# Queries and keys of two batch entries in seven block products of eight, in a decoder layer written out by slots

## The chip, the cores and the metric

The kernel runs on one core of one Trainium2 chip. The core has a tensor engine (TensorE, "PE" in a profile, with its weight loads listed as "PEld"), a vector engine (VectorE, DVE), a scalar engine (ScalarE, ACT), GpSimd (POOL), and a queue that issues most DMAs (SyncE, SP). [...] The metric is device time in microseconds (us); lower is better.

## The reference

The reference is one pre-norm decoder layer on 16 batch entries of 128 tokens with 256 features, all in float32. Cut to what matters:

```
x = x + self_attention(layernorm(x))            # 16 heads of 64, biases on Q, K, V and output
x = x + cross_attention(layernorm(x), context)  # 16 heads of 16, keys masked
x = x + experts(layernorm(x))                   # 8 experts of 512, all computed, scaled by a gate

Q = einsum('btd,hkd->bthk', x, W_Q) + b_Q       # 256 features -> 16 * 64 = 1024
K = einsum('btd,hkd->bthk', x, W_K) + b_K
scores = einsum('bqhk,bshk->bhqs', Q, K) / 8
```

The change concerns Q and K of the self attention. In the kernel they are needed transposed: 1024 rows, as 8 chunks of 128, by 128 tokens of an entry. The 256 features are two blocks of 128, so a chunk of one entry is the sum of two 128x128x128 products: 16 products for the queries of an entry and 16 for its keys.

## The kernel before

**Stages.** A first part computes both attentions entry by entry; a second one computes the experts over 2048 tokens in four groups of 512. Between them lies a short tail that finishes the cross attention of the last two entries and computes some hidden values of the first expert. The expert part already forms its products in the seven-of-eight manner, with the helpers `combined` (sums of weight blocks) and `right` (differences of token blocks).

**Slots.** The first part is a pipeline of 16 slots, one per batch entry. Slot `s` does the self attention of entry `s`, most of the cross attention of entry `s - 1`, the end of that of `s - 2`, the norm for the experts of `s - 3`, and the projections (queries, keys, values) of entry `s + 1`. Slots 0 to 2 lack the parts whose entry would be negative. Slot 15 has no next entry; six steps `pre_hidden` (two matmuls of 512 columns each, hidden values of the first expert) stand in the places of the projections there.

**What sets the order.** The order on PE, DVE, ACT and POOL is written out by hand. Each step has a name with a due time in the table `DUE` (for slot 0 some have another in `FIRST_DUE`). A step of slot `s` is due at `s * SLOT + DUE[name]`. All steps are put in one heap and issued by due time; an engine then executes its instructions strictly in that order. The due times are only an order, the real times are made by the chip. SP's DMAs are not under this table's order of engines, but are issued where the steps call them.

The names that the prediction uses, with what they do:

- `S0`, `S1`: scores of the two halves of the heads (line 465). `max0`, `max1`: their maxima, on DVE (line 351). `ex0a`, `ex0b`, `ex1a`, `ex1b`: the exponentials, on ACT (line 357), four heads each. `r..`: reciprocals of the sums, on DVE (line 368). `mul..`: the products with them, on POOL (line 372).
- `T1a1` to `T1b2`: transposes of the probabilities on PE (line 387), with a copy out of PSUM, named with a final `e`. `T2..`: the same for the cross attention of entry `s - 2`.
- `SVa`, `SVb`: probabilities times values; `atT0`, `atT1`: their evictions with a bias, on DVE. `SO`: the output projection; `xsSO`: its addition to the residual `xs`, on DVE. `bn`, `root`: statistics and inverse root; `xn`, `xn3`: normalised rows for the cross attention and for the experts. `LNx`, `LN3`, `LN1`: their transposes on PE; `LNxc`, `LN3c`, `LN1c`: the copies on ACT. `xn1`: normalised rows for the next self attention. `st0` to `st11`: statistics of entries 4 to 15, taken in slot 0; `late`: their roots. `ab..`: addition of an output bias to `xs`, on POOL.
- `cvr`, `ck`, `CQ`, `CS`, `CV`, `CO`: value rows, keys, queries, scores, values and output of the cross attention; `msk0`, `msk1`: its masks, on DVE; `c` before a softmax name marks the cross attention's (`cmax0`, `cex0a`). `cvre`, `cke`, `q2T`, `at2T`, `xsCO`: their evictions. `cross`: some small set-up for it in slot 0.
- `q0`, `q1`, `k0`, `k1`: queries and keys of entry `s + 1`, chunks 0 to 3 and 4 to 7 (line 410); `q0e`, `q1e` evict the queries on DVE, `ke0`, `ke1` the keys on ACT. `v0`, `v1`: the values (line 449), `ve0`, `ve1` their copies on ACT.

**PSUM.** All results of matmuls except scores are put in tiles of one bank from the pool `ps_mm`, which has four:

```
ps_mm = both.enter_context(
    tc.tile_pool(name="ps_mm", bufs=4, space=bass.MemoryType.PSUM, side="right")
)
```

The four are handed out in turn, so a step that takes a new tile needs the tile of four allocations earlier to have been read. Scores have a pool of their own with two tiles of two banks.

**Weights.** `wq`, `wk` and `wv` lie in the buffers `k0`, `k1` and `k2` of the pool `keep`, whose fourth one, `k3`, is unused until the first `pre_hidden`. Two of four parts of the experts' first weights (`w1_0`, `w1_1`) are loaded at the start.

Of the kernel before, what the change touches and what calls it, by code (L numbers as in the profile page):

```python
# [18 lines left out]
P = 128  # L19
# [32 lines left out]
SLOT = 28.2  # L52
DUE = dict(
    S0=0.0, S1=1.0, max0=1.2, LNx=2.0, cvr=2.22, max1=2.34, LNxc=2.42, ex0a=2.72, T2b1=3.09,
    T2b2=3.53, T2b1e=3.72, q0=3.96, cvre=4.09, T2b2e=4.32, ex0b=4.44, r0a=4.92, mul0a=5.2,
    T2a1=5.7, ex1a=5.81, q0e=5.9, T2a2=6.14, r0b=6.5, k0=6.57, T2a1e=6.63, mul0b=6.78, ex1b=7.19,
    T2a2e=7.23, r1a=7.83, mul1a=8.11, CQ=8.31, ke0=8.56, r1b=8.76, mul1b=9.13, v0=9.18, q2T=9.38,
    xn1=10.44, T1a1=10.9, ab1=11.04, ve0=11.1, T1a2=11.34, T1a1e=11.54, T1b1=11.77, T1a2e=12.14,
    T1b2=12.21, LN1=12.64, T1b1e=12.74, LN1c=13.06, CS=13.08, T1b2e=13.34, msk0=14.23, SVa=14.25,
    SVb=15.15, atT0=15.42, msk1=16.02, CV=16.15, q1=17.2, atT1=17.21, at2T=17.81, cmax0=18.15,  # L60
    LN3=18.94, SO=19.16, q1e=19.29, LN3c=19.36, cex0a=19.66, cmax1=19.89, cex0b=21.03,
    cr0a=21.36, cmul0a=22.23, cex1a=22.4, cr0b=22.6, CO=22.61, xsSO=22.81, bn=23.22,
    cmul0b=23.25, v1=23.47, xsCO=23.72, cex1b=23.78, cr1a=24.06, bn3=24.19, cmul1a=24.34,
    root=24.79, k1=25.19, ve1=25.39, ke1=27.13, cr1b=27.14, ck=27.19, xn=27.27,
    cmul1b=27.42, xn3=27.77, cke=28.26, ab2=28.44, early0=6.65, early1=6.7, early=7.9,
    cross=13.9, st0=14.3, st1=14.8, st2=15.6, st3=16.2, st4=17.4, st5=17.9, st6=18.4, st7=18.9,
    st8=20.0, st9=20.5, st10=21.0, st11=21.5, late=31.7,
)

FIRST_DUE = dict(  # L70
    fk0=-11.4, fq0=-9.5, fk0e=-9.4, fq0e=-7.7, fk1=-7.2, norm1=-7.0, S0=-5.4, fk1e=-5.3, fq1=-4.4,
    max0=-4.0, ex0a=-2.7, fLN=-2.65, fq1e=-2.6, fv0=-2.3, fLNc=-1.4, r0a=-1.32, ex0b=-1.3,
    mul0a=-1.2, S1=-0.6, fv0e=0.1, r0b=0.15, mul0b=0.2, max1=0.4, fv1=0.41, ex1a=1.65, fv1e=3.0,
    r1a=3.1, mul1a=3.2, ex1b=3.6, cvre=5.0, r1b=5.1, mul1b=5.2, fab0=5.5, fab1=6.5,
)
PRE_STEPS = ("q0", "k0", "v0", "q1", "v1", "k1")
# [4 lines left out]
def decoder_layer(  # L81
# [147 lines left out]
    for i in range(2):  # L229
        load_w1(i, we1)  # L230


    bk1 = const.tile([P, C1], F32, tag="bk1", name="bk1")
    xnT = const.tile([P, KD, NT], F32, tag="xnT", name="xnT")
# [148 lines left out]
    def transposed(w, prT, n, name):  # L383

        tr = psum_mm("tr_p").rearrange("p (j t) -> p j t", j=4)
        for j in range(4):
            nc.tensor.transpose(tr[:, j, :], w["pr"][:, 4 * n + j, :], ident)  # L387
        due(name, nc.vector.tensor_copy, prT[:, 4 * n : 4 * n + 4, :], tr)
# [7 lines left out]
    def self_norm_transposed(b, name="LN1c"):  # L396
        xnT1 = ap.tile([P, KD, 1, T], F32, tag="xnT1", name="xnT1")
        transpose_tokens([entry.pop(("xn1", b))], xnT1, name)
        entry["xnT1", b] = xnT1

    def project(b, w, n, tag):

        mm = psum_mm("mm_qk").rearrange("p (c t) -> p c t", c=4)
        if n == 0:
            entry[tag, b] = ap.tile([P, C1, T], F32, tag=tag, name=tag)
        xnT1 = entry["xnT1", b]
        for i in range(4):
            c = 4 * n + i
            for k in range(KD):
# [3 lines left out]
                    xnT1[:, k, 0, :],  # L413
# [3 lines left out]
        return entry[tag, b], mm  # L417

    def queries(b, n, name="q{}e"):
# [4 lines left out]
            qT[:, 4 * n : 4 * n + 4, :],  # L424
# [33 lines left out]
    def self_scores(b, half):  # L458

        qT, kT = entry["qT", b], entry["kT", b]  # L460
        sc = psum_sc("sc1")
        for c in range(4):
            for j in range(2):
# [3 lines left out]
                    qT[r, 4 * half + c, :],  # L467
                    kT[r, 4 * half + c, :],
# [314 lines left out]
    def slot(s):  # L783
# [23 lines left out]
        if s + 2 < B:  # L807
            at("xn1", self_norm, s + 2)
            at("ab1", add_bias, s + 2, BO1)
            at("LN1", self_norm_transposed, s + 2)  # L810
        if s + 1 < B:
            for n in range(2):
                at(f"q{n}", queries, s + 1, n)
                at(f"k{n}", keys, s + 1, n)
                at(f"v{n}", values, s + 1, n)
        else:
            for n, name in enumerate(PRE_STEPS):
                copy = nc.vector.tensor_copy if name[0] == "q" else nc.scalar.copy
                out = f"q{name[1]}e" if name[0] == "q" else f"{name[0]}e{name[1]}"
                at(name, pre_hidden, n, copy, out)  # L820
        if s == 0:
            for n in range(2):
# [3 lines left out]
                at(f"fab{n}", add_bias, n, BO1)  # L826

# [5 lines left out]
            at("fLN", self_norm_transposed, 1, "fLNc")  # L833
# [447 lines left out]
```

## Time and profile before

| | us |
|---|---|
| median of 3 runs | 867.79 (867.68 to 867.98) |
| the profiled execution | 868.2 |
| its span, first to last instruction | 866.1 |
| first `S0` of slot 0, of slot 1, of slot 2 | 13.39, 42.70, 67.17 |
| `S0` of slots 14 and 15 | 403.13, 430.93 |
| end of slot 15 | 458.36 |

Times inside the span count from its start. In a group of instructions, "x16" counts instructions of the engine; a float32 product of 128x128 weights is two of them on PE, so 8 products are x16. Busy times of neighbouring instructions overlap a little: the time that one takes in a dense row is read from start to start. A line of a timeline gives the start, the duration, the engine, the line of the kernel, the operation, what it writes and reads, the shape, the count, and in brackets the idle time before it with what ended that.

### The profile page before, as it was taken

To read this page: it belongs to the slowest core of one execution; us is meant where nothing else is said; L and a number is where in the kernel's file an instruction comes from. 1 tells how busy PE (TensorE), PEld (TensorE's weight loads), DVE (VectorE), ACT (ScalarE), POOL (GpSimd) and SP (SyncE) were. 2 spreads that over 40 slices of the span, in tenths; PEclk is the share of its full clock that TensorE was granted. 3 is DMA by queue.
4 is the path that set the end of the run, shared out by engine and by line. 5 is a ranking of instruction groups with operands and counts; after the bars stand their busy time and mean duration, and the time that the engine had idled before them with its cause. 6 is when DMAs were issued, how large, how long until landed. Compare 5 with 4: busy or idle time off the path is not lost.

```text
span 866.1 us, 15987 instructions
## 1 busy us (share of the span) xinstructions
PE 856.7 (99%) x5962; PEld 718.1 (83%) x5962; DVE 627.8 (72%) x1517; ACT 429.1 (50%) x1629; POOL 166.5 (19%) x179
## 2 busy tenths in 40 slices
PE   8999999999999999999999999999999999999997
PEld 7888888888888888888875557888888888888886
DVE  4887787778878787878777587786656766576656
ACT  3365765567565755576554713343344334343342
POOL 5133423343233423343321100000000000000000
PEclk9999999999999999999999999999999999999999
DMA  8700000000000000000041100000000000000000
GB/s 228 250 2 14 2 13 2 2 13 2 13 2 2 13 2 2 14 2 2 28 173 45 48 1 1 1 13 13 0 1 1 25 1 0 1 13 13 1 0 25
DMA packets 18318, 21.29 MB, mean 25 GB/s; under 512 B 9585, under 2 KB 13697, under 8 KB 17601
## 3 DMA queue, kind: packets, MB, share of 16 engines
q1 hardware_dynamic: 17728, 19.93, 7.3%
q8 instruction: 47, 0.77, 0.4%
q0 software_dynamic: 368, 0.30, 0.2%
q14 instruction: 31, 0.25, 0.1%
q10 hardware_dynamic: 144, 0.04, 0.0%
HBM read 18.16 MB, written 2.10 MB: 23 GB/s over the span
## 4 chain that ended last, share of the span: by engine, by line
PE 90%; DVE 6%; ACT 1%; DMA 1%; issue 1%; SPq 0%; POOL 0%; DVEq 0%; POOLq 0%
PE y L1025 19%; PE mm_qk L410 12%; PE mm_o L509 6%; PE tr_p L387 6%; PE mm_v L449 6%; PE he L1025 5%; PE hf L1025 5%; PE ha L1025 5%; PE sc L465 4%; PE po L489 3%; PE mm_h L773 3%; PE hb L1025 3%; PE sc L599 2%; PE po L638 2%; PE y L915 2%; PE mm_q L577 2%
## 5 line engine op out<-in xcount | busy, mean ns | idle before, releaser
L372 POOL TENSOR_TENSOR cpr<-cpr,rinv 128x512 f32<-128x512 f32 x64 | 68.5, 1071 | 220.2 <-DVE rinv L368 219.8
L357 ACT ACTIVATE cpr<-sc,nmax 128x128 f32<-128x128 f32 x256 | 89.9, 411 | 11.6 <-DVE nmax L351 11.6
L357 ACT ACTIVATE pr<-sc,nmax 128x128 f32<-128x128 f32 x256 | 90.9, 418 | 2.6 <-DVE nmax L351 2.6
L372 POOL TENSOR_TENSOR pr<-pr,rinv 128x512 f32<-128x512 f32 x64 | 65.8, 1040 | 74.0 <-DVE rinv L368 73.2
L351 DVE TENSOR_REDUCE nmax<-sc 128x8 f32<-128x1024 f32 x64 | 76.5, 1216 | 1.0 <-PE sc L465 1.0
L1054 ACT ACTIVATE h<-u,colv 128x256 f32<-128x256 f32 x56 | 28.4, 508 | 93.6 <-DVE u L1041 91.7
L1055 DVE TENSOR_TENSOR c<-u,hf 128x256 f32<-128x256 f32 x56 | 23.5, 420 | 69.3 <-PE hf L1025 69.1
L278 ACT COPY xnT<-tr_x 128x256 f32<-128x256 f32 x43 | 16.0, 373 | 109.2 <-PE tr_x L336 109.2
L410 PEld LDWEIGHTS mm_qk<-xnT,wk 128*128 128x128 f32 x512 | 60.9, 192 | 8.4 <-issue 4.1
L1025 PE MATMUL hf<-xt,w 128*128 128x256 f32 x224 | 66.8, 380 | 0.4 <-DVE u L1040 0.4
L1025 PE MATMUL ha<-xnT,w 128*128 128x256 f32 x224 | 66.6, 379 | 0.0
L1025 PE MATMUL y<-t,w 128*128 128x256 f32 x224 | 66.6, 380 | 0.0
L357 ACT ACTIVATION_READ_ACCUMULATOR pr<-sc,nmax 128x1 f32 x256 | 65.9, 257 | 0.0
L357 ACT ACTIVATION_READ_ACCUMULATOR cpr<-sc,nmax 128x1 f32 x256 | 64.4, 252 | 0.0
L410 PE MATMUL mm_qk<-xnT,wq 128*128 128x128 f32 x512 | 64.0, 278 | 0.0
L410 PE MATMUL mm_qk<-xnT,wk 128*128 128x128 f32 x512 | 62.5, 275 | 0.9 <-ACT xnT L262 0.5
L1038 ACT COPY u<-ha 128x256 f32<-128x256 f32 x56 | 20.9, 372 | 84.9 <-PE ha L1025 84.9
L410 PEld LDWEIGHTS mm_qk<-xnT,wq 128*128 128x128 f32 x512 | 59.8, 192 | 3.1 <-issue 2.9
L449 PE MATMUL mm_v<-wv,xnT 128*128 128x512 f32 x128 | 60.3, 593 | 0.0
L509 PE MATMUL mm_o<-wo,atT 128*128 128x256 f32 x256 | 57.9, 379 | 0.0
L1025 PE MATMUL y<-h,w 128*128 128x256 f32 x224 | 57.6, 379 | 0.0
L278 DVE COPY prT<-tr_p 128x512 f32<-128x512 f32 x64 | 39.7, 682 | 19.3 <-PE tr_p L387 19.3
(174 smaller groups left out, 1879.8 us busy)
## 6 DMA issues: line engine op xcount, KB each, us to landing
w<-in_w SPq DMA_DIRECT2D x8, 1024.0 KB, 5.5
ctx<-in_ctxT SPq DMA_DIRECT2D x8, 256.0 KB, 2.7
out_x<-ot SPq DMA_DIRECT2D x8, 256.0 KB, 2.1
xs<-in_x SPq DMA_DIRECT2D x3, 512.0 KB, 5.2
wk<-in_wk SPq DMA_DIRECT2D x2, 512.0 KB, 6.9
wq<-in_wq SPq DMA_DIRECT2D x2, 512.0 KB, 7.7
wv<-in_wv SPq DMA_DIRECT2D x2, 512.0 KB, 9.7
wo<-in_wo SPq DMA_DIRECT2D x1, 1024.0 KB, 8.9
```

The costliest lines, as they stand in the source:

```text
L278: f(*a)
L351: nc.vector.tensor_reduce(w["nmax"], sc, AX.X, ALU.max, negate=True)
L357: nc.scalar.activation(w["pr"][:, i, :], sc[:, i, :], AF.Exp, bias=w["nmax"][:, i : i + 1], scale=1.0, accum_out=sums[:, j : j + 1],)
L372: nc.gpsimd.tensor_tensor(four, four, w["rinv", n].unsqueeze(2).broadcast_to([P, 4, T]), ALU.mult)
L387: nc.tensor.transpose(tr[:, j, :], w["pr"][:, 4 * n + j, :], ident)
L410: nc.tensor.matmul(mm[:, i, :], w[:, k, c * P : (c + 1) * P], xnT1[:, k, 0, :], start=(k == 0), stop=(k == KD - 1),)
L449: nc.tensor.matmul(mm, entry["xnT1", b][:, k, 0, :], wv[:, k, f], start=(k == 0), stop=(k == KD - 1),)
L465: nc.tensor.matmul(sc[:, j, c * T : (c + 1) * T], qT[r, 4 * half + c, :], kT[r, 4 * half + c, :], start=True, stop=True,)
L489: nc.tensor.matmul(po[j * DH1 : (j + 1) * DH1, c, :], v[:, h * DH1 : (h + 1) * DH1], prT[:, 4 * j + c, :], start=True, stop=True,)
L509: nc.tensor.matmul(mm[:, :D], atT[:, c, :], wo[:, c, :], start=(c == 0), stop=(c == C1 - 1))
L1025: nc.tensor.matmul(out, left[p // q][n - 1][:, p % q], rights[n - 1], **flags)
L1054: nc.scalar.activation(h[:, 1, 1], u[:, 3], AF.Gelu, bias=col(B1 + 2 * p + 1))
```

## The change

Queries and keys of entries 0 and 1 are projected as before. From entry 2 on two entries `b0` and `b0 + 1` are projected together. For the four chunks of one half, the two chunk parities and the two feature blocks form a 2x2 matrix of 128x128 weight blocks (for each of two pairs of chunks), the two feature blocks and the two entries a 2x2 matrix of token blocks. Their product, eight block products, is formed from seven, with sums of weight blocks made once in slot 0 (`weight_sums`, steps `w0` and `w1`; the sums need the weights changed in place, and the keys' scale is put into the weights) and differences of token blocks made once per pair (`pair_factors`, step `tf`).

Slot `s` does half `s % 2` of the pair that begins at `s + 2 - s % 2`: 14 products for queries and 14 for keys, in slots 0 to 13. The seven products lie in two banks: products 1 and 6 in the halves `a` and `b` of one, 7 and 5 in `f` and `e` of the other; products 2, 4 and 3 are added to `a`, `f` and `e` later. The steps on PE are `q1x`, `q1y`, `q2x`, `q2y` and the same with `k`. Their sums are formed on ACT (`qu0`, `qc00`: two pieces of 128x128 each) and DVE (`qu1`, `qu2`, `qu3`, `qc1` of 128x256, `qc0` as two of 128x128).

The norms and transposes for the next self attention are done for two entries in every second slot. The four `T1` copies move from DVE to ACT. The value projection `v1` comes before `v0`, the cross and expert steps have new places, and `SLOT` becomes 27.34 with 7.5 more for slot 0. Slot 0 does the plain queries and keys of entry 1, both weight sums and the first half of the pair (2, 3). Two of the six early hidden steps move from slot 15 to slot 14. The sums lie in the unused buffer `k3` and in the buffer of `w1_1`, whose load is therefore issued in slot 14. The pool of normalised rows has 4 buffers instead of 6. `qT` and `kT` become half tiles with three and two buffers.

```diff
-SLOT = 28.2
+SLOT = 27.34
+EXTRA = 7.5
 DUE = dict(
...
+    S0=0.0, S1=1.0, max0=1.2, LNx=2.0, LN3=2.22, max1=2.34, LNxc=2.42, cvr=2.44, LN3c=2.72,
+    ex0a=3.02, T2b1=3.31, T2b2=3.75, T2b1e=3.94, CQ=4.18, cvre=4.39, T2b2e=4.54, ex0b=4.74,
+    T2a1=5.05, r0a=5.14, q2T=5.27, mul0a=5.42, T2a2=5.49, T2a1e=5.69, q1x=5.92, ex1a=6.11,
+    T2a2e=6.28, xn1=6.5, q1y=6.82, r0b=6.88, mul0b=7.16, qu0=7.49, r1a=7.69, v1=7.72, ex1b=7.99,
+    mul1a=8.19, qu1=8.21, qu2=8.64, qu3=9.07, LN1=9.44, r1b=9.56, ve1=9.64, q2x=9.66,
+    mul1b=9.84, LN1c=10.1, q2y=10.11, qc00=10.4, tf=10.62, ab1=11.0, qc1=11.21, CS=11.23,
+    qc0=11.56, msk0=12.38, T1a1=12.4, T1a2=12.84, T1a1e=13.03, T1b1=13.27, T1a2e=13.53,
+    msk1=13.57, T1b2=13.71, T1b1e=14.03, CV=14.24, T1b2e=14.53, cmax0=14.76, SVa=15.29,
+    at2T=15.9, cex0a=16.08, SVb=16.19, cmax1=16.24, CO=17.19, atT0=17.38, cex0b=17.45,
+    atT1=17.98, k1x=18.05, cr0a=18.58, xsCO=18.71, cex1a=18.82, cmul0a=18.86, k1y=18.95,
+    cr0b=19.05, bn3=19.18, SO=19.85, cmul0b=19.88, ku0=20.2, cr1a=20.4, cex1b=20.7, cmul1a=20.9,
+    ku1=20.92, ku2=21.35, ku3=22.03, cr1b=22.38, cmul1b=22.9, k2x=23.3, xsSO=23.5, k2y=23.75,
+    bn=23.91, kc00=23.95, root=24.51, ck=24.65, v0=25.52, cke=25.72, kc1=26.86, kc0=27.21,
+    ve0=27.44, xn=27.65, xn3=27.98, ab2=28.15, st0=14.3, st1=14.8, st2=15.6, st3=16.2, st4=17.4,
+    st5=17.9, st6=18.4, st7=18.9, st8=20.0, st9=20.5, st10=21.0, st11=21.5, late=38.1,
 )
 FIRST_DUE = dict(
...
+    ke0=8.56, v0=9.18, xn1=10.44, T1a1=10.9, ab1=11.04, ve0=11.1, T1a2=11.34, T1a1e=11.54,
+    T1b1=11.77, T1a2e=12.14, T1b2=12.21, LN1=12.64, T1b1e=12.74, LN1c=13.06, T1b2e=13.34,
+    w0=13.6, cross=13.7, tf=13.9, SVa=14.25, SVb=15.15, atT0=15.42, q1=17.2, atT1=17.21,
+    k1=18.0, SO=19.16, q1e=19.29, ke1=19.6, w1=20.0, xsSO=22.81, bn=23.22, v1=23.47, root=24.79,
+    ck=25.2, ve1=25.39, q1x=26.9, cke=27.0, xn=27.27, qu0=27.4, q1y=27.8, qu1=28.2, ab2=28.44,
+    k1x=28.7, qu2=28.8, qu3=29.2, ku0=29.3, ku1=29.85, q2x=30.5, q2y=30.95, qc00=31.0,
+    k1y=31.85, qc1=32.0, qc0=32.4, k2x=32.8, ku2=32.9, ku3=33.3, kc00=33.3, k2y=33.4, kc1=34.5,
+    kc0=34.9,
 )
-PRE_STEPS = ("q0", "k0", "v0", "q1", "v1", "k1")
+PRE_STEPS = (
+    (14, "q1x", "qu1"), (14, "k1x", "kc00"),
+    (15, "q1x", "qu1"), (15, "v1", "ve1"), (15, "k1x", "kc00"), (15, "v0", "ve0"),
+)
+ON_ACT = ('T1a', 'T1b')
...
-    for i in range(2):
-        load_w1(i, we1)
+    load_w1(0, we1)
+    places = (
+        keep.tile([P, 4 * 512], F32, tag="k3", name="sums_q"),
+        we1.tile([P, 4 * 512], F32, tag="w1_1", name="sums_k"),
+    )
...
+        if s == 0:
+            return FIRST_DUE[name] if name in FIRST_DUE else DUE[name]
+        return EXTRA + s * SLOT + DUE[name]
...
-        due(name, nc.vector.tensor_copy, prT[:, 4 * n : 4 * n + 4, :], tr)
+        copy = nc.scalar.copy if name[:3] in ON_ACT else nc.vector.tensor_copy
+        due(name, copy, prT[:, 4 * n : 4 * n + 4, :], tr)
...
+    def weight_sums(n):
+        f = slice(n * 512, (n + 1) * 512)
+        nc.vector.tensor_scalar_mul(wk[:, :, f], wk[:, :, f], DH1 ** -0.5)
+        for x, w in (("q", wq), ("k", wk)):
+            a = w[:, :, f].rearrange("p k (q i c) -> p i k q c", i=2, c=P)
+            more = places["qk".index(x)][:, n * 768 : (n + 1) * 768]
+            paired[x, n] = combined(a, more.rearrange("p (n q c) -> p n q c", n=3, c=P))
+
+    def pair_factors(b0):
+        t = places[b0 // 2 % 2][:, 1536:].rearrange("p (n t) -> p n t", n=4)
+        x4 = [[tokens(b0 + i, k) for i in range(2)] for k in range(2)]
+        paired[b0] = right(t, x4[0][0], x4[0][1], x4[1][0], x4[1][1])
+
+    def paired_steps(x, b0, n):
...
+        def product(m, out, clears=False):
+            for q in range(2):
+                nc.tensor.matmul(
+                    out[:, q, :], paired[x, n][m - 1][:, q], paired[b0][m - 1],
+                    start=clears and q == 0, stop=True, skip_group_check=True,
+                )
+        def first():
+            v["a"], v["b"] = bank()
+            product(1, v["a"], clears=True)
+            product(6, v["b"])
+            u = v["u"] = ap.tile([P, 2, 2, T], F32, tag="su", name="su")
+            due(f"{x}u0", with_bias, u[:, 0], v["a"], 1)
+            due(f"{x}u1", nc.vector.tensor_tensor, u[:, 0], u[:, 0], v["b"], ALU.add)
+        def second():
+            v["f"], v["e"] = bank()
+            product(7, v["f"], clears=True)
+            product(5, v["e"])
...
+            due(f"{x}u2", nc.vector.tensor_tensor, u[:, 1], u[:, 0], v["f"], ALU.add)
+            due(f"{x}u3", nc.vector.tensor_tensor, out[1][:, 1], u[:, 1], v["e"], ALU.add)
+        def third():
+            product(2, v["a"])
+            due(f"{x}c00", with_bias, v["out"][0][:, 0], v["a"], 0)
+        def fourth():
+            product(4, v["f"])
+            product(3, v["e"])
+            u, out = v["u"], v["out"]
+            due(f"{x}c1", nc.vector.tensor_tensor, out[0][:, 1], u[:, 0], v["f"], ALU.add)
+            def rest():
+                for q in range(2):
+                    nc.vector.scalar_tensor_tensor(
+                        out[1][:, 0, q], v["e"][:, q], b01[:, q : q + 1], u[:, 0, q],
+                        ALU.add, ALU.add,
+                    )
+            due(f"{x}c0", rest)
+        return {f"{x}1x": first, f"{x}1y": second, f"{x}2x": third, f"{x}2y": fourth}
...
+        bs = [2, 3] if s == 0 else [s + 3, s + 4] if s % 2 and s + 4 < B else []
+        for b in bs:
+            at("xn1", self_norm, b)
+            at("ab1", add_bias, b, BO1)
+        if bs:
+            at("LN1", self_norm_transposed, bs)
+            at("tf", pair_factors, bs[0])
+        b0 = s + 2 - s % 2
+        if b0 < B:
+            for x in "qk":
+                for name, f in paired_steps(x, b0, s % 2).items():
+                    at(name, f)
         if s + 1 < B:
             for n in range(2):
-                at(f"q{n}", queries, s + 1, n)
-                at(f"k{n}", keys, s + 1, n)
                 at(f"v{n}", values, s + 1, n)
-        else:
...
+        if s == B - 2:
+            at("S0", load_w1, 1, we1)
...
         if s == 0:
...
+                at(f"q{n}", queries, 1, n)
+                at(f"k{n}", keys, 1, n)
+                at(f"w{n}", weight_sums, n)
...
+    for n, b in enumerate((col(BQ1, C1), bk1)):
+        nc.vector.tensor_sub(bqk01[:, n, :], b[:, 0::2], b[:, 1::2])
```

The helpers `combined` (four sums on DVE: `s1`, `s2` from it, `s4` from that, and one in place) and `right` (four differences) move up from the expert part unchanged in what they compute.

## The prediction

> **What bounds the kernel now.** I read the page first, for the engines' shares and the granted clock.
>
> ```profile
> span 866.1 us, 15987 instructions
> PE 856.7 (99%) x5962; PEld 718.1 (83%) x5962; DVE 627.8 (72%) x1517; ACT 429.1 (50%) x1629; POOL 166.5 (19%) x179
> PE   8999999999999999999999999999999999999997
> DVE  4887787778878787878777587786656766576656
> PEclk9999999999999999999999999999999999999999
> ```
>
> TensorE is busy in every slice at full clock, so a matmul left out is time saved, unless another engine then comes last. The view by stretches, one per group of slots, shows how near that is.
>
> ```profile
> 13.39:42.70 29.31, 28.48 (x210) 22.66 (x209) 21.93 (x75) 11.94 (x51) 6.25 (x7) 1.00 0.83 238
> 42.70:67.16 24.46, 24.38 (x209) 20.73 (x208) 20.35 (x54) 16.62 (x82) 8.61 (x9) 1.00 0.01 1
> 95.03:403.13 308.10, 308.10 (x2883) 266.73 (x2882) 245.27 (x540) 191.33 (x904) 108.48 (x111) 1.00 0.02 6
> 403.13:430.93 27.80, 27.80 (x261) 24.03 (x261) 21.80 (x49) 17.03 (x83) 9.15 (x10) 1.00 0.01 1
> 430.93:458.36 27.43, 27.43 (x214) 19.86 (x213) 21.64 (x49) 16.23 (x77) 9.04 (x9) 1.00 0.54 192
> ```
>
> These are slots 0, 1, 3 to 13, 14 and 15: length, then busy time of PE, PEld, DVE, ACT, POOL. Slots 3 to 13 have PE busy throughout: 28.0 us each, DVE 22.3, ACT 17.4. Last comes the timeline of PE, DVE and POOL.
>
> ```profile
> 239.04 1.95 PE L410 MATMUL mm_qk<-xnT,wq 128*128 128x128 f32 x16
> 240.83 1.04 PE L387 MATMUL tr_p<-ident,cpr 128*128 128x128 f32 x8
> 437.52 1.88 PE L773 MATMUL mm_h<-xnT,w 128*128 128x512 f32 x4
> 439.24 1.05 PE L577 MATMUL mm_q<-xnT,wx 128*128 128x128 f32 x8
> 29.32 2.48 DVE L278 COPY prT<-tr_p 128x512 f32<-128x512 f32 x4
> 30.06 0.44 PE L336 MATMUL tr_x<-ident,xn 128*128 128x128 f32 x2 [0.67 <-DVE prT L278]
> 40.85 0.40 DVE L278 TENSOR_TENSOR xs<-mm_o,xs 128x256 f32<-128x256 f32 x1
> 42.70 2.06 PE L465 MATMUL sc<-kT,qT 64*128 64x128 f32 x32
> 231.53 1.04 POOL L372 TENSOR_TENSOR cpr<-cpr,rinv 128x512 f32<-128x512 f32 x1 [0.52 <-DVE rinv L368]
> 232.01 0.58 DVE L315 TENSOR_SCALAR var<-mv 128x2 f32<-128x2 f32 x1
> ```
>
> Eight projection products (16 PE instructions) take 240.83 - 239.04 = 1.79 us from start to start, 0.224 each; an early hidden step takes 1.72. The transposes at 30.06 waited for the copy that freed a PSUM bank four allocations earlier: the `ps_mm` ring of four is handed on strictly and whole, and a late DVE copy stops TensorE. That is the mechanism I fear.
>
> **TensorE's work alone.** Slots 1 to 13 have 28 products instead of 32: 4 x 0.224 = 0.895 us less. Slots 2 to 13 give 12 x 0.895 = -10.7, slot 1 -0.9. Slot 0 keeps the 32 for entry 1 and adds 28: +6.3. Slot 14 loses 32 (7.16) and gets two hidden steps (3.44): -3.7. Slot 15 gives those two up: -3.4. Together -12.5 us, the ceiling.
>
> **DVE, ACT and POOL in a full slot.** Removed from DVE: two qT evictions and four prT copies of 128x512, spaced 0.60: -3.6. Added: eight sums of 128x256 (the `u` rows last 0.42, follow each other at 0.34, or 0.46 where one needs the one before): 3.2; four of 128x128 (nearest, the `lg` row of 0.29): about 1.0; four factor differences every second slot: 0.5. Net +1.1, so DVE 23.4 of 27.1. ACT keeps eight 128x128 key or query pieces and gets four copies (0.60 each by the `v` row, spaced 0.5): 19.5 of 27.1. Both fit, so I walked one odd slot in the new order, TensorE dense, S0 at 0, a result usable 0.2 after TensorE moves on (CQ left it at 244.38, its DVE reader began at 244.58) and 0.05 after any other engine. The tight places:
> - T2a1 needs the bank of cvr, whose copy stands behind ex0a on ACT, behind max0 on DVE: max0 1.2 to 2.4, ex0a to 3.85, copy to 4.2; TensorE arrives at 5.1.
> - q2x needs qu0, qu1 (8.4; asked at 10.0); q2y needs qu2, qu3 (9.3; 10.5).
> - T1a2 needs the bank that qc0 empties. qc0 stands behind tf and so behind LN1c: done 12.6, asked 12.9. Lead 0.2, the smallest.
> - CO needs at2T (16.65; 17.1), k1y the bank that atT0 frees (18.45; 18.85), SO atT1 (19.05; 19.7). All stand behind the two masks, 1.28 each.
> - k2y needs ku3 (22.5; 23.7). The chain from SO through bn, root and both norms now has kc1 and kc0 in it, and S0 follows SO by 4.05 instead of 5.35 (229.69 to 235.04); it loses xsCO and bn3, which move before SO. max0 can start 5.15 after SO ends, 1.1 after S0 starts: just in time.
> Queued behind each DVE wait are the reciprocals, and POOL behind those; mul1b ends at 11.0, T1b2 asks at 13.7. I take no stall but 0.05 per slot, +0.6; bounds 0 and 0.5 per slot. `var` shows what can lengthen this: 0.58 us beside a POOL product, 0.15 in the chain without one (496.04).
>
> [...]
>
> **Slot 0, where the gain goes.** DVE is dense from the norm at 29.0 to xsSO at 40.85. The change takes the four prT copies out (-2.4), adds a second norm (+0.35), two `weight_sums` and tf. One `weight_sums` is a scaling of 128x1024 (nearest: the immediate-scalar 128x128 row of 0.227, less its fixed 0.15, times eight, gives 0.77; at one element per step like `xn` it is 1.2) and eight sums of 128x256, alternately 0.46 and 0.33: 3.2. That is 3.95, bounds 3.3 and 4.7. Due 13.6 and 20.0, both stand before xsSO (22.81), as do the twelve statistics. So xsSO starts at 40.85 - 2.4 + 0.35 + 7.9 + 1.0 = 47.7, and is done at 48.1.
>
> TensorE: SO waits for atT0, behind w0, cross, tf and two statistics: about 37.3 instead of 36.0. SO ends 40.8, v1 42.5, ck 43.5, q1x 44.4. q1y is the fourth allocation after SO and needs its bank, which xsSO frees: 48.15, a stall of 3.75. Then bn and root precede qu1 on DVE, 3.36 after xsSO starts as at 40.85 to 44.21: qu1 51.1 to 51.4, qu3 to 52.3. q2x writes the bank qu1 reads: 51.45; q2y 52.4 to 53.3; k1y, k2x to 54.6; k2y after ku2, ku3: 55.25 to 56.15. S0 of slot 1 starts at 56.15 instead of 42.70: +13.4, of which 6.3 is work and 7.2 stalls. If the two halves of a bank could be used by two engines at once, q2x and q2y could go earlier: +11.9. I take 13.4, since every bank in this trace is read after its last matmul and rewritten after its last reader.
>
> [...]
>
> **Slot 1** has no T2, CV or CO to cover DVE. tf, qc1 and qc0 end at 11.9 where T1a2 asks at 11.5; masks, maxima and both atT follow, so SO starts at 17.4 instead of 16.5; k2y waits for ku3. 25.4 instead of 24.46: +0.9.
>
> **Slots 14, 15, tail.** The same walk finds TensorE dense there: SO at 17.8, atT1 at 17.2. In the tail the T2 copies wait for both norms as now (the 0.65 stall before 460.49); +0.3 for S0 following SO sooner.
>
> **Hidden, with their cover.** `bqk01`: two tiny DVE ops of 0.15, in DVE's 4.8 us wait for the first projection. The `w1_1` load (5.5 us, on SP) moves to slot 14 and is read in the tail some 55 us later; nothing else on SP is due. Uncovered, either would cost its own length. POOL gets nothing new.
>
> **Sum:** -10.7 + 13.4 + 0.9 - 3.7 - 3.4 + 0.6 + 0.3 = -2.6. The profiled execution took 868.2 (span 866.1 and 2.1 around it), 0.4 over the median of 867.79; the sum gives 865.6 against the one, 865.1 against the other.
>
> **Rivals.**
> - *A, slot 0 does not queue.* If DVE reaches xsSO by 44.4, or q1y has another bank, only the work remains: -12.5 + 0.9 = 856. For it: PE was 97% busy in slot 0. Against: DVE's order by due times, and its dense timeline from 29.0. Chance 0.12.
> - *B, full slots lose 0.3 each* at T1a2, CO or k1y, because tf or a norm runs beside POOL: 12 x 0.3 instead of 0.6, 868.1. For: leads of 0.2 to 0.4. Against: POOL's cross products end earlier than before, so `var` and `xn` lose their delay. Chance 0.20.
> - *C, slower: the chain from SO to the next max0.* If it keeps the length of before (6.5 us from SO's end, POOL beside it) with kc1 and kc0 in it, LN3 and cvr's copy come too late, and T2a1 waits 0.5 per slot: 6 us instead of 0.6, 870.5. From 0.4 per slot on the kernel is slower by over 0.2%. For: S0 follows SO 1.3 sooner. Against: xsCO and bn3 leave the chain. Chance 0.15.
> - *Forecast*: 0.53, 861.5 to 867 by the bounds on slot 0 (11.0 to 15) and the slots.
>
> **Numbers.** 0.2% (1.7 us) is about what this measurement tells from no change: 866.1 to 869.5. Forecast: faster 0.43, same 0.10. A: faster. B: faster 0.05, same 0.09, slower 0.06. C: same 0.02, slower 0.13. Faster 0.60, same 0.21, slower 0.19. The range 859 to 870.5 cuts most of A and half of C.
>
> **What would show it.** Slots 2 to 13 of 27.1 to 27.2 us with PE busy throughout; S0 of slot 1 at 56; a PE wait of about 4 us at q1y put down to DVE xs; DVE's weight sums of 3.9 us each; slot 14 near 24.1. Wrong, if slot 0 ends near 50, or if full slots show repeated waits on DVE or ACT at T1a2, CO or T2a1.

## The result, and the profile after

The changed kernel takes 872.27 us (median of 6 runs, 871.35 to 872.84), the kernel before, on the same chip, 867.97 (867.68 to 868.21). The ratio is 1.0048 with a 95% interval of 1.0035 to 1.0061: slower by half a per cent, where 865.1 and "faster" were predicted, and outside the range of 859.0 to 870.5. The profiled execution took 872.84, its span is 871.0.

The page of the changed kernel, engines and slices:

```profile
span 871.0 us, 16083 instructions
PE 851.9 (98%) x5850; PEld 706.5 (81%) x5850; DVE 636.8 (73%) x1641; ACT 461.7 (53%) x1686; POOL 165.3 (19%) x179
PE   8979999999999999999999999999999999999997
DVE  4878787888888888877776587786656765576655
PEclk9989999999999999999999999999999999999999
```

TensorE has 112 instructions less and is busy 4.8 us less, as meant, but the span grew by 4.9. The third slice (43 to 65 us) has both a 7 in the PE row and an 8 in the row of the granted clock, which before was 9 throughout. The view by stretches, for slots 0, 1, 3 to 13, 14, and one odd and one even slot (length, then busy PE, PEld, DVE, ACT, POOL, then the granted clock):

```profile
13.64:59.23 45.59, 38.05 (x267) 31.61 (x266) 33.73 (x109) 18.36 (x67) 8.22 (x9) 0.93 0.46 128
59.23:86.45 27.22, 25.08 (x203) 20.02 (x203) 22.93 (x62) 18.66 (x84) 9.67 (x10) 1.00 0.02 7
113.28:415.14 301.86, 300.75 (x2794) 255.53 (x2793) 248.37 (x625) 213.28 (x940) 106.68 (x109) 1.00 0.03 7
415.14:439.37 24.23, 24.23 (x205) 18.16 (x204) 17.51 (x40) 17.44 (x78) 9.03 (x9) 1.00 0.09 36
223.14:251.17 28.03, 27.75 (x258) 23.43 (x257) 23.96 (x61) 19.69 (x86) 10.49 (x11) 1.00 0.03 6
251.17:278.23 27.06, 27.06 (x254) 23.07 (x253) 21.46 (x55) 19.15 (x85) 9.03 (x9) 1.00 0.02 6
```

From these and the starts of `S0` the difference falls apart as follows:

| part | predicted | measured | how |
|---|---|---|---|
| slot 0 | +13.4 | +16.3 | 45.59 against 29.31 |
| slot 1 | +0.9 | +2.8 | 27.22 against 24.47 |
| slots 2 to 13 | -10.1 | -7.3 | 328.69 (86.45 to 415.14) against 335.96 |
| slot 14 | -3.7 | -3.6 | 24.23 against 27.80 |
| slot 15 and all behind | -3.1 | -3.5 | the rest of the span |

The remaining 0.25 of the 4.9 lie ahead of the first `S0`, which came at 13.64 instead of 13.39. The last two terms were right or nearly so. Slot 0 missed by 2.9, slot 1 by 1.9, the full slots by 2.8. The timeline shows where to look first, in slot 0 (PE and DVE) and in an odd full slot (POOL, DVE and PE):

```profile
46.94 0.61 PE L533 MATMUL mm_qk<-sums_k 128*128 128x128 f32 x4
52.42 1.22 PE L533 MATMUL mm_qk<-xnT,wq 128*128 128x128 f32 x4 [4.88 <-DVE su L304]
53.44 1.19 PE L533 MATMUL mm_qk<-sums_k,wq 128*128 128x128 f32 x4
48.60 0.41 DVE L304 TENSOR_TENSOR xs<-mm_o,xs 128x256 f32<-128x256 f32 x1
51.95 0.94 DVE L304 TENSOR_TENSOR su<-su,mm_qk 128x256 f32<-128x256 f32 x2
...
233.19 1.04 POOL L398 TENSOR_TENSOR pr<-pr,rinv 128x512 f32<-128x512 f32 x1 [0.17 <-DVE rinv L394]
234.19 1.51 POOL L366 TENSOR_TENSOR xs<-xs,rowv 128x256 f32<-128x256 f32 x2
234.30 0.81 DVE L434 TENSOR_TENSOR sums_k<-xnT 128x128 f32<-128x128 f32 x1
235.04 0.81 DVE L435 TENSOR_TENSOR sums_k<-xnT,sums_k 128x128 f32<-128x128 f32 x1
235.89 0.29 DVE L436 TENSOR_TENSOR sums_k<-xnT,sums_k 128x128 f32<-128x128 f32 x1
235.57 2.23 PE L413 MATMUL tr_p<-ident,pr 128*128 128x128 f32 x16
238.74 1.97 PE L635 MATMUL po<-prT,v 128*64 128x128 f32 x32
240.92 1.13 PE L804 MATMUL mm_o<-wx_vo,at2T 128*128 128x256 f32 x4 [0.21 <-DVE at2T L304]
```

Three things are to be seen. TensorE stands idle for 4.88 us at `q2x`, waiting for `qu1`, which on DVE stands behind `xsSO`, `bn`, `root` and `xn`. Behind that gap a group of four instructions lasts 1.22 where it lasted 0.61 just before. And two of the subtractions of `tf` last 0.81 beside POOL's instructions, where the one after POOL's end lasts 0.29; `CO` (line 804) then waits for `at2T`. The second one is seen plainly by stretches, before and behind the gap (the clock is the third number from the end):

```profile
44.62:47.55 2.93, 2.92 (x26) 2.73 (x24) 2.79 (x11) 2.02 (x6) 0.00 (x0) 1.00 0.00 0
52.42:57.00 4.58, 4.58 (x21) 4.53 (x22) 2.12 (x6) 0.63 (x2) 0.42 (x1) 0.50 0.00 0
```

26 instructions in 2.93 us before the gap, 21 in 4.58 behind it, at a granted clock of 0.50.

### The profile page after: what moved, and what is told of

The parts are those of the page before. It is cut to its first block, busy times and chain, and to the rows that moved or that the text cites. A ratio compares the mean times of both kernels' runs of the same rounds, so it can differ in the third digit from the quotient of the medians.

```text
span 871.0 us, 16083 instructions
## 1 busy us (share of the span) xinstructions
PE 851.9 (98%) x5850; PEld 706.5 (81%) x5850; DVE 636.8 (73%) x1641; ACT 461.7 (53%) x1686; POOL 165.3 (19%) x179
## 4 chain that ended last, share of the span: by engine, by line
PE 83%; DVE 12%; ACT 2%; issue 1%; DMA 1%; SPq 0%; DVEq 0%
PE y L1161 18%; PE mm_qk L533 9%; PE mm_o L655 6%; PE mm_v L595 6%; PE he L1161 5%; PE hf L1161 5%; PE ha L1161 5%; PE tr_p L413 5%; PE sc L611 4%; PE mm_h L919 3%; PE hb L1161 3%; PE po L635 2%; PE mm_o L804 2%; DVE sc L304 2%; PE y L1073 2%; PE mm_q L723 2%
## 5 line engine op out<-in xcount | busy, mean ns | idle before, releaser
L383 ACT ACTIVATE pr<-sc,nmax 128x128 f32<-128x128 f32 x256 | 92.8, 430 | 2.6 <-DVE nmax L377 2.6
L398 POOL TENSOR_TENSOR cpr<-cpr,rinv 128x512 f32<-128x512 f32 x64 | 65.3, 1041 | 141.5 <-DVE rinv L394 141.4
L383 ACT ACTIVATION_READ_ACCUMULATOR pr<-sc,nmax 128x1 f32 x256 | 68.8, 269 | 0.0
L655 PEld LDWEIGHTS mm_o<-wo,atT 128*128 128x128 f32 x256 | 47.6, 190 | 9.7 <-DVE atT L304 3.0
L1161 PEld LDWEIGHTS ha<-xnT,w 128*128 128x128 f32 x224 | 42.6, 190 | 7.1 <-issue 1.0
L1161 PEld LDWEIGHTS hf<-xt,w 128*128 128x128 f32 x224 | 42.4, 190 | 6.7 <-DVE u L1176 1.0
L304 ACT COPY prT<-tr_p 128x512 f32<-128x512 f32 x64 | 33.2, 598 | 27.6 <-PE tr_p L413 27.5
L1161 PEld LDWEIGHTS y<-h,w 128*128 128x128 f32 x224 | 42.6, 190 | 5.8
L1161 PEld LDWEIGHTS y<-t,w 128*128 128x128 f32 x224 | 41.9, 190 | 6.2 <-issue 0.8
```

Source lines behind the costliest of these rows:

```text
L304: f(*a)
L383: nc.scalar.activation(w["pr"][:, i, :], sc[:, i, :], AF.Exp, bias=w["nmax"][:, i : i + 1], scale=1.0, accum_out=sums[:, j : j + 1],)
L398: nc.gpsimd.tensor_tensor(four, four, w["rinv", n].unsqueeze(2).broadcast_to([P, 4, T]), ALU.mult)
L655: nc.tensor.matmul(mm[:, :D], atT[:, c, :], wo[:, c, :], start=(c == 0), stop=(c == C1 - 1))
L1161: nc.tensor.matmul(out, left[p // q][n - 1][:, p % q], rights[n - 1], **flags)
```

## The experiments

Two theories came out of this: in slot 0 DVE is the bound, and the long wait that it causes also costs TensorE its clock; in the odd full slots `tf` is stretched by POOL and makes TensorE wait. The rivals were that neither is on the path. The diffs of due times show the changed entries alone. The runs were made on several chips, on which the kernel before took 867.96 to 868.41; the ratios, each against the kernel before on the same chip, allow for that, the medians in us do not.

### Keeping TensorE busy through the gap

21 products of the identity, which nobody reads, stand between `k1x` and `q2x`.

```diff
-    k1x=28.7, qu2=28.8,
+    k1x=28.7, warm=28.75, qu2=28.8,
+            def warm():
+                sc = psum_sc("warm")
+                for i in range(21):
+                    nc.tensor.matmul(sc[:, 0, :T], ident, ident, start=True, stop=True)
+            at("warm", warm)
```

> The changed kernel with 21 products of the identity with itself, which nothing reads, put on TensorE between k1x and q2x of slot 0, where it stood idle for 4.88 us. Theory (the clock): the granted clock of 0.50 in the 4.6 us after that gap is the gap's own doing, so with the gap filled the five groups after it take 0.45 us each instead of 0.9 and S0 of slot 1 starts near 57.2 instead of 59.2; the whole is 1.5 to 2.3 us faster than the changed kernel, 870.0 to 870.8. Rival (the queue alone): the groups are slow because their operands come late, the clock is a side effect, S0 of slot 1 stays at 59.2 and the time at 872.3. What DVE does before qu1 is the same in both, so neither expects more than 2.5.

Measured: 871.07 (870.65 to 871.72), ratio to before 1.0031 (1.0019 to 1.0043). Slot 0 takes 43.64 instead of 45.59. Its timeline on TensorE:

```profile
47.35 4.85 PE L987 MATMUL warm<-ident 128*128 128x128 f32 x42
52.40 0.71 PE L533 MATMUL mm_qk<-xnT,wq 128*128 128x128 f32 x4 [0.20 <-DVE su L304]
53.93 0.61 PE L533 MATMUL mm_qk<-xnT,sums_q 128*128 128x128 f32 x4
```

`q2x` starts at 52.40 as before, so the wait itself is the same, but behind it the groups last 0.61 again and the clock is 1.00 throughout. The whole gained 1.2, less than the 1.5 to 2.3 expected (1.5 by the ratios); the slot shows the gain as forecast. The idle gap therefore cost twice: 4.9 us of standing still and 1.95 of slow work after it.

### tf behind qc0

The four subtractions of `tf`, which last 0.45, 0.81, 0.81 and 0.29 in the odd slot shown above, move behind `qc0`.

```diff
-    qc00=10.4, tf=10.62, ab1=11.0, qc1=11.21, CS=11.23, qc0=11.56, msk0=12.38,
+    qc00=10.4, ab1=11.0, qc1=11.21, CS=11.23, qc0=11.56, tf=12.0, msk0=12.38,
```

> The changed kernel with one due time changed: tf at 12.0, behind qc0 and ahead of msk0, instead of 10.62. [...] Behind qc0 they take about 0.29 each; odd slots fall from 27.9 to 28.0 to about 27.4, slot 1 from 27.2 to about 26; the whole is 3 to 5 us faster than the changed kernel, 867.3 to 869.3. Rival (DVE is simply full in odd slots): the work is only put behind something else, the masks start no earlier, and the time stays within 1 us of 872.3.

Measured: 869.28 (868.99 to 869.79), ratio 1.0008 (0.9999 to 1.0017). Slots 3, 5, 7, 9 and 11 take 27.49 instead of 27.87 to 28.03, slot 1 26.54 instead of 27.22, even slots 27.06 as they were. `tf` was on the path. Whether POOL was the reason is a separate question, taken up below.

### The weight sums on GpSimd

```diff
+    def combined(a, more, eng=None):        # called from weight_sums with nc.gpsimd
-        nc.vector.tensor_add(s1, a[1][0], a[1][1])
+        eng.tensor_add(s1, a[1][0], a[1][1])
...
```

> The changed kernel with the sixteen sums of weight_sums on POOL, which is idle from 26 to 60 us, instead of DVE; the two scalings stay on DVE. Theory (DVE's queue bounds slot 0): DVE loses 6.5 us ahead of xsSO and qu1, TensorE's gap of 4.88 us and the low clock behind it go, S0 of slot 1 starts at 50 to 51.5 instead of 59.2, and the whole is 7.5 to 9.5 us faster than the changed kernel, 863 to 865. Rival (contention): the sums on POOL, some 0.75 each, hold up DVE's roots and norms as the products of POOL did with var, and q1x of slot 0 waits for them; then S0 of slot 1 comes at 54 or later and the gain is below 5.

Measured: 865.9 (865.38 to 867.2), ratio 0.9973 (0.9962 to 0.9983): faster than the kernel before. Slot 0 takes 39.82 instead of 45.59.

```profile
30.82 0.73 POOL L425 TENSOR_TENSOR sums_q<-wq 128x256 f32<-128x256 f32 x1
32.63 0.81 DVE L435 TENSOR_TENSOR sums_k<-xnT 128x128 f32<-128x128 f32 x1
47.40 0.71 PE L534 MATMUL mm_qk<-xnT,wq 128*128 128x128 f32 x4 [1.25 <-DVE su L304]
```

A sum takes 0.73 on POOL against 0.42 on DVE, yet the wait at `q2x` falls from 4.88 to 1.25 and no slow group follows it. DVE pays something back: `tf` beside POOL's sums lasts 0.81 for a subtraction again, and `cross` and `tf` together take 4.6 us (30.20 to 34.82) instead of 1.9 (34.74 to 36.66). That may be why the gain of 6.4 us is less than the theory's 7.5 to 9.5; it was not tested by itself.

### The T1 copies back on DVE

```diff
-ON_ACT = ('T1a', 'T1b')
+ON_ACT = ()
```

> The changed kernel with the four T1 copies back on DVE, which undoes one part of the change. Theory (DVE is the scarce engine of the new order): 2.4 us more on DVE in each slot; slot 0 gets 2.4 longer, odd slots, whose DVE is busy 23.9 of 28.0, 1 to 2 longer, even ones up to 1: 880 to 895. Rival (the copies on ACT cost the small waits before CV and SV): full slots get 0.15 to 0.3 shorter, and the time falls to 868 to 871.

Measured: 902.86 (902.66 to 903.82), ratio 1.0399 (1.0381 to 1.0416). That is above the 880 to 895 expected. Even slots take 28.73, odd ones 30.26, which is 1.7 and 2.4 more; the four copies are 2.4 us of DVE (0.60 each). So 70% of the time that DVE is given in an even slot, and all of it in an odd one, reaches the end of the slot, although DVE was only 21.46 of 27.06 us busy in an even one. A share of busy time says little about an engine that stands in the chain with fixed order.

### Order alone in slot 0

```diff
-    st0=14.3, st1=14.8, st2=15.6, st3=16.2, st4=17.4, st5=17.9, st6=18.4, st7=18.9,
+    st0=17.3, st1=17.5, st2=17.7, st3=17.9, st4=19.4, st5=19.5, st6=19.6, st7=19.7,
-    bn=23.22, root=24.79, xn=27.27, ab2=28.44,
+    bn=29.9, root=29.95, xn=32.5, ab2=33.0,
```

> The changed kernel with the same VectorE work in slot 0 in another order, nothing moved to another engine: the statistics st0 to st7 stand behind atT1 and q1e, and bn, root and xn stand behind qu1, qu2, qu3 and ku1. All of the shortfall of slot 0 is told apart into order and amount. Theory (the fault is the order: 3.0 us of bn, root and xn between xsSO and qu1, and 1.1 us of statistics ahead of atT0): SO waits about 1.0 less, qu1 starts right behind xsSO at about 49.0 instead of 51.95, the gap ahead of q2x falls from 4.9 to about 2, too short for the half clock of 2.3 us that followed it, root then delays qc1 by up to 0.8: S0 of slot 1 at 54 to 55 instead of 59.2, the whole at 867 to 869. Rival (the fault is the amount of VectorE work, 45 us of slot 0 with no slack for it): what is put behind qu1 is late again at qc1, ku2 and LNx, S0 of slot 1 or of slot 2 gains under 2 us, the whole at 870 to 872.

Measured: 869.23 (868.97 to 870.46), ratio 1.0015 (1.0006 to 1.0025). Slot 0 takes 42.65 instead of 45.59: the order is worth 2.9 us, a little under the theory's range and above the rival's limit of 2. The gap at `q2x` became 2.9, not 2, and the clock fell all the same. Timeline and stretches:

```profile
45.31 0.61 PE L533 MATMUL mm_qk<-sums_k 128*128 128x128 f32 x4
48.83 1.22 PE L533 MATMUL mm_qk<-xnT,wq 128*128 128x128 f32 x4 [2.91 <-DVE su L304]
```

```profile
43.00:45.90 2.90, 2.90 (x26) 2.73 (x24) 2.76 (x8) 2.02 (x6) 0.00 (x0) 1.00 0.00 0
48.83:54.50 5.67, 5.61 (x24) 5.27 (x24) 5.20 (x20) 0.64 (x3) 0.69 (x1) 0.50 0.00 0
```

My expectation that a gap of some 2 us would be too short for the low clock, as the 1.97 ahead of `SO` was in the changed kernel, was not put to the test by it; the gap of 2.91 was followed by the low clock.

### A due time that changes nothing

```diff
-    ab1=11.0,
+    ab1=16.0,
```

> The changed kernel with one edit: from slot 1 on, GpSimd's two additions ab1 (128x256, two SBUF inputs) are due at 16.0 instead of 11.0, so none of them runs beside the four subtractions tf on VectorE. VectorE's order and work are untouched. Theory (tf is stretched by GpSimd's work beside it): tf's third subtraction falls from 0.81 to about 0.29 and the second to between 0.3 and 0.8 (mul1b still ends beside it), qc0 ends about 0.6 earlier in odd slots and they take about 27.4 to 27.5 instead of 27.9 to 28.0, even slots unchanged; the whole 2.5 to 3.5 us shorter, 869 to 870. Rival (tf is late by VectorE's own queue): durations of tf and odd slots unchanged, 872.

Measured: 871.62 (871.52 to 872.16), ratio 1.0043 (1.0028 to 1.0058), and odd slots of 27.87 to 28.02: the changed kernel's own times. POOL has nothing else due between 11.0 and 16.0, so the additions kept their place in its queue and ran beside `tf` as before. Neither theory is touched by it. A due time is only a place in an order.

### ab1 behind cmul0b

```diff
-    ab1=11.0,
+    ab1=19.9,
```

> The changed kernel with one edit: from slot 1 on, GpSimd's two additions ab1 are due at 19.9, behind its cmul0b, so that they change places in GpSimd's queue with the three products cmul0a, cmul0b and do not run beside tf (the edit to 16.0 left the queue in the same order, and so the program as it was). VectorE's order and work are untouched. Theory (tf is stretched by GpSimd's work beside it): the second and third of tf's subtractions fall from 0.81 to between 0.28 and 0.5, qc0 ends 0.5 to 0.9 earlier in odd slots and they take 27.5, as with tf behind qc0; even slots unchanged at 27.06; the whole 2 to 3.5 us shorter, 869 to 870. Rival (tf is late by VectorE's own queue): tf's durations and the odd slots unchanged, 872.

Measured: 869.46 (868.56 to 870.6), ratio 1.0011 (1.0001 to 1.002). Odd slots take 27.49, slot 1 26.14. In the odd slot, with DVE's order as in the changed kernel:

```profile
233.00 0.45 DVE L433 TENSOR_TENSOR sums_k<-xnT 128x128 f32<-128x128 f32 x1 [0.82 <-ACT xnT L304]
233.37 0.28 DVE L434 TENSOR_TENSOR sums_k<-xnT 128x128 f32<-128x128 f32 x1
233.57 0.28 DVE L435 TENSOR_TENSOR sums_k<-xnT,sums_k 128x128 f32<-128x128 f32 x1
```

The subtractions that lasted 0.81 last 0.28, though DVE does the same work in the same order and only POOL's additions are elsewhere. That is the cause shown: POOL beside it, not DVE's own queue.

### Two mends together

The sums on GpSimd and `tf` behind `qc0`, both edits as above.

> Both earlier mends at once: the sixteen sums of the weights' blocks on GpSimd, and tf behind qc0. Theory (two faults in different slots, independent of each other): 865.9 less 3.0 gives about 862.9; S0 of slot 1 at 52.5, slot 1 at 26.4, odd slots 27.5. Rival (one mend uses up the slack that the other needs): less than 1.5 us below 865.9.

Measured: 863.88 (863.38 to 864.49), ratio 0.9955 (0.9938 to 0.9972). Slot 0 takes 38.98, slot 1 26.47, odd slots 27.49. That is 2.0 below the sums alone (1.6 by the ratios) where 3.0 was expected and 1.5 was the rival's limit, so the whole times decide little. The slots do: slot 1 gives 0.65 and each of five odd slots 0.38, 2.5 together, in slots that the sums do not touch. There the two faults are independent. One line of slot 0 matters for what follows; it is `q1y`, waiting for `xsSO`:

```profile
44.07 0.68 PE L534 MATMUL mm_qk<-sums_k,wq 128*128 128x128 f32 x4 [0.77 <-DVE xs L304]
```

### Half of the sums on GpSimd, and the order

The order of the fifth experiment, `tf` behind `qc0`, and only the second half's sums on GpSimd:

```diff
-            paired[x, n] = combined(a, more.rearrange(...))
+            paired[x, n] = combined(a, more.rearrange(...), nc.gpsimd if n else None)
```

> The edit of order in slot 0, tf behind qc0 from slot 1 on, and the sums of the second half of the weights (w1, eight subtractions and additions, its scaling stays) on GpSimd, while the first half stays on VectorE. VectorE has then 3.4 us less in slot 0, and GpSimd's sums stand where VectorE runs no subtraction with two SBUF inputs. Theory (slot 0 is bound by VectorE alone): no wait of TensorE over 1 us is left in slot 0 behind SO, no low clock; S0 of slot 1 at 50 to 51, slot 1 at 26.5 to 27, the whole at 860 to 861.5. Rival (something else, such as the order of the banks or the copies on ScalarE, holds slot 0): S0 of slot 1 stays at 52 or later and the whole at 862.5 or more.

Measured: 867.55 (866.32 to 868.41), ratio 0.9995 (0.9986 to 1.0004); slot 0 takes 41.80. The theory's numbers failed and the rival's came (`S0` of slot 1 at 54.68), but for neither of the reasons that it named. POOL, DVE and PE in slot 0:

```profile
32.64 0.79 POOL L426 TENSOR_TENSOR sums_q<-sums_q,wq 128x256 f32<-128x256 f32 x1
32.77 0.94 DVE L425 TENSOR_TENSOR sums_k<-wk 128x256 f32<-128x256 f32 x1
35.37 0.41 DVE L428 TENSOR_TENSOR wk<-wk 128x256 f32<-128x256 f32 x1
38.36 3.72 PE L656 MATMUL mm_o<-wo,atT 128*128 128x256 f32 x16 [2.54 <-DVE atT L304]
53.59 0.71 PE L534 MATMUL mm_qk<-sums_k,wk 128*128 128x128 f32 x4 [2.86 <-DVE kT L304]
54.68 3.66 PE L612 MATMUL sc<-kT,qT 64*128 64x128 f32 x32
```

I had not seen that the queries' half of POOL's sums waits for nothing and runs at once, beside DVE's own sums. Those last 0.83 to 0.94 instead of 0.42, the whole of `w0` 6.5 instead of 4.85, and `SO` waits 2.54. Later `root`, now ahead of `qc1`, `ku2` and `ku3`, delays them, and `k2y` waits 2.86; the low clock then falls on the scores, 3.66 instead of 2.06.

### Lighter slot 0, and root behind ku3

First `cross` behind `atT1` and the statistics of entries 12 to 15 moved to slots 2 to 5, with a root of their own (`later`) in slot 6, on top of the two mends:

```diff
-    w0=13.6, cross=13.7,
-    st8=20.0, st9=20.5, st10=21.0, st11=21.5, late=38.1,
+    w0=13.6, cross=17.5,
+    st8=72.08, st9=99.42, st10=126.76, st11=154.10, late=38.1, later=181.44,
```

> On top of the two mends together (863.9): in slot 0 the preparation of the masks (cross) stands behind atT1 instead of ahead of it, and the statistics of entries 12 to 15 leave slot 0 for slots 2 to 5, one each ahead of qc1 where VectorE idles 1.2 to 1.7 us, with their own root in slot 6. Theory (VectorE alone still holds slot 0: 0.95 at SO, 0.8 at q1y and 1.25 at q2x are its waits): these three waits shrink by 2.5 to 3 us together, S0 of slot 1 at 49.5 to 50.5, the slots from 2 on lose under 0.6 us in all, the whole at 860.5 to 862. Rival (the waits are latency chains on VectorE and ScalarE that keep their length, or slots 2 to 6 give the gain back): 863 or more.

Measured: 863.39 (862.93 to 863.81), ratio 0.9943 (0.993 to 0.9955). The waits at `SO` and `q1y` went, but the one at `q2x` grew from 1.25 to 1.79, since `bn`, `root` and `xn` still stood ahead of `qu1`; slot 0 takes 38.47, and slot 6, with the new root in it, gives 0.85 back (27.90). As much as the rival said. So that order was changed too:

```diff
-    root=24.79, xn=27.27, ab2=28.44, later=181.44, tf=12.0, ab1=11.0,
+    root=33.35, xn=33.4, ab2=33.45, later=208.78, tf=10.62, ab1=19.9,
```

> On top of the last kernel: in slot 0 root and xn stand behind ku3 instead of between xsSO and qu1; from slot 1 on ab1 stands behind cmul0b and tf is back ahead of qc0 (the two mends of tf are worth the same in odd slots, and ab1 behind gave 0.3 more in slot 1); the late root moves from slot 6, where it cost 0.85, to slot 7. Theory (q2x's wait of 1.8 is nothing but root and xn standing ahead of qu1): that wait falls to 0.1 or less, S0 of slot 1 comes at 49.5 to 50, slot 1 takes 26.1 to 27.2 as max0 may be 1.2 late behind root and kc0, slot 7 loses under 0.5, the whole at 861 to 862.5. Rival (the chain of the products themselves, product, ScalarE, VectorE, product, sets the end of slot 0): the wait moves to k2y or S0, S0 of slot 1 stays at 51 or later, the whole at 863 or more.

Measured: 862.5 (861.78 to 863.49), ratio 0.9932 (0.9918 to 0.9945). Slot 0 takes 36.71, 1.76 less (`S0` of slot 1 came at 51.31, beyond the 50 expected, but this run's `S0` of slot 0 came at 14.60, against 12.97 in the run before):

```profile
45.72 0.61 PE L534 MATMUL mm_qk<-sums_k 128*128 128x128 f32 x4
46.22 0.71 PE L534 MATMUL mm_qk<-xnT,wq 128*128 128x128 f32 x4
50.22 0.71 PE L534 MATMUL mm_qk<-sums_k,wk 128*128 128x128 f32 x4 [0.52 <-DVE var L341]
```

The wait at `q2x` is gone and none above 0.52 took its place. The term for slot 7 was wrong: the late root costs 1.32 there (28.81), not under 0.5. This is the best version found, 0.7% faster than the kernel before. It has the same products as the changed kernel; what differs is which engine forms the sums and in which order DVE and POOL work.

## Why the prediction was wrong

**TensorE's work alone**: slots 14 and 15 came as computed. In the full slots, with `tf`'s stall gone, slots 2 to 13 still take 326.6 us, 9.4 less than before instead of 10.7. TensorE shows no wait in these slots (27.49 busy of 27.49), so the 1.4 us lie in its own sequence. The step "12 x 0.895" itself was right: added up from start to start over the twelve slots, the products of queries and keys take 10.9 us less in the run with `tf` behind `qc0`. What the prediction put at nothing is that the other work of TensorE takes another time in the new order. Most of it is in the sixteen `T1` transposes, here in one slot of before (first two lines) and of that run:

```profile
218.09 1.91 PE L387 MATMUL tr_p<-ident,pr 128*128 128x128 f32 x16
219.83 0.38 PE L336 MATMUL tr_x<-ident,xn 128*128 128x128 f32 x2
233.38 1.97 PE L413 MATMUL tr_p<-ident,pr 128*128 128x128 f32 x16
235.27 1.08 PE L784 MATMUL po<-cprT,v 128*32 128x128 f32 x32
```

From their start to the next step they take 1.89 instead of 1.74, 1.8 us in twelve slots; the other steps together give 0.3 back. The transposes now stand between steps with weights of other shapes, 32x128 ahead of them and 128x32 behind; that this is the reason was not tested and stays open.

**Stalls of full slots**, "+0.6": no run shows the 0.05 per slot that it was added up from, which was my estimate; the runs showed 0.38 to 0.54 in each of five odd slots in its place, 2.1 in all, and nothing in even ones. The cause is POOL's work beside `tf`: a 128x128 subtraction lasted 0.28 without it, in the run with `ab1` behind `cmul0b`, and 0.81 with it. The two `ab1` follow `mul1b` at once, so the stretch goes on through two of the four subtractions. At `T1`, behind `qc0`, where the walk had its smallest lead of 0.2, four of the five lost 0.1 (0.26 in the slot shown); the larger part, 0.28 in each, was lost at `CO`, which the walk had given a lead of 0.45: the masks behind `qc0` start late and with them `at2T`. Rival B, a loss of 0.3 per full slot because tf or a norm runs beside POOL, named this mechanism, and the mean loss against the ceiling is 0.29 (3.5 in twelve slots, 2.1 of stall and the 1.4 of sequence); its 868.1 had slots 0 and 1 at their forecast. Rival C, the chain from `SO` to `max0`, did not occur: `max0` started 1.2 behind `S0`.

**Slot 0**: the queue on DVE was right in order and nearly in size. `xsSO` started at 48.6 where 47.7 was forecast; the first `weight_sums` took 4.85 instead of 3.95 because its scaling (1.22 against 0.69 for the second) and its first sum (0.95 against 0.42) ran beside POOL's `ab1`; the second took 3.8. Two steps failed. "q1y is the fourth allocation after SO and needs its bank" is wrong: `q1y` ran at 45.5, ahead of `xsSO` and without a wait. The description of the pool that the prediction rests on, a ring handed on in turn, does not hold: in the program as built, `q1y` has the bank of `v1`, and that of `SO` goes to `k1y`. In the run of both mends, with the same order on TensorE, `q1y` did wait 0.77 for `xsSO`; so counting allocations does not tell which step needs which bank. Rival A's "or q1y has another bank" came true, and the wait stayed: the wait of about 4 us that the prediction put at `q1y` appeared at `q2x`, for `qu1`, and there the other half of the argument held: `q2x`, which writes one half of a bank, began at 52.42, released by `qu1` on DVE, which reads the other half and began at 51.95. The sum hardly changed by that, as `qu1` was the next limit in the walk too (51.1 forecast, 51.95 measured). The step that was missing is the clock. A wait of 3.75 us was forecast and what TensorE does after it was costed at full speed; it ran at 0.50 for 4.6 us, and that is 1.95 of the 2.9 us missed in this slot. Most of the rest is `xsSO`, which came 0.65 later than forecast when counted from the slot's start.

**Slot 1**, "+0.9", was +2.75. With `ab1` away from `tf` it is 26.14, so 1.1 of the 1.9 missed is again POOL beside `tf`: there all three products of POOL and both additions follow one another, and the first three subtractions last 0.79 to 0.81. The remaining 0.8 were not tested; what that run still shows in slot 1 are waits for DVE, the longest of them `SO`'s 0.54 for `atT`.

**The sign**: four terms were missed in the same direction, 2.9 in slot 0, 1.9 in slot 1, and in the full slots 1.5 of stalls (2.1 against 0.6) and 1.4 of TensorE's own sequence. The range ended at 870.5 because each rival was priced alone, with slots 0 and 1 at their forecast; the loss of the full slots, that of slot 1 and that of the clock came together, and each was under 3 us.

## What to carry to other kernels

Waits of TensorE of 2.86, 2.91 and 4.88 us came here with 3.4 to 5.9 us of work at a clock of 0.50; where a forecast contains such a wait, price what follows it so, or fill the wait with products that nobody reads, as 21 of them kept the clock at 1.00 here. Before moving work between VectorE and GpSimd, lay their timelines side by side: VectorE's subtractions and sums that overlapped GpSimd's work took two to three times as long here (0.81 against 0.28, 0.83 to 0.95 against 0.42), and shifting either queue cost nothing (869.28 and 869.46 against 872.27). Where a step gets its PSUM bank from a pool, read from a trace whom it waits for instead of counting. In a hand-ordered pipeline ask not how busy an engine is but what stands ahead of the instruction that the critical engine waits for.

## What the runs showed of the hardware that was not expected

- After an idle gap of 4.88 us the granted clock was 0.50 for 4.6 us of work, after one of 2.91 us for 5.9 us. It had fallen within the gap, 2.66 and 2.00 us after TensorE had stopped, and the low clock lasted 6.8 us both times (first two lines below: the changed kernel, and the run of the order alone). After a gap of 2.86 us it fell too, but only 1.1 us after TensorE had started again, and for 3.41 us (last line). A gap of 2.54 us was followed by full clock (`SO`, 3.72 us as in the changed kernel), as were those of 1.97 (`SO` of the changed kernel) and 1.25 (`q2x` with all sums on GpSimd). So the length of a gap alone did not tell how long the low clock lasts.

```profile
50.21:57.04 6.83, 4.62 (x21) 4.57 (x22) 4.03 (x15) 0.63 (x2) 0.72 (x1) 0.50 0.00 0
47.92:54.74 6.82, 5.79 (x25) 5.44 (x26) 6.04 (x23) 0.88 (x3) 0.72 (x1) 0.50 0.00 0
54.68:58.09 3.41, 3.41 (x33) 3.41 (x32) 2.17 (x4) 0.00 (x0) 0.00 (x0) 0.50 0.00 0
```

- Beside a running GpSimd instruction, VectorE's 128x128 subtraction of two SBUF operands lasted 0.81 (odd slot of the changed kernel) instead of 0.28 (the run with `ab1` behind `cmul0b`), a 128x256 sum 0.83 to 0.94 (half of the sums on GpSimd) and 0.95 (changed kernel) instead of 0.42, and the in-place scaling of 128x1024 1.22 instead of 0.69 (both in slot 0 of the changed kernel). GpSimd pays too: its own 128x256 sums went from 0.72 to at most 0.91 (half of the sums on GpSimd), but an addition `ab1` of the same size, 0.73 alone, took 1.18 beside that scaling in the changed kernel and 1.77 in the run with half of the sums on GpSimd, where the scaling kept its 0.69.
